# One transpose per group for the remaining columns with copies by DMA, and q and k in three chunks at a pitch of ten rows

## The chip, the cores and the metric

The kernel runs on one core of a Trainium2 chip. The metric is the time of one launch on the device, in microseconds; the kernel is fp32 throughout.

## The reference

The input x has 32 samples of 128 tokens and 144 channels, and each sample has a conditioning vector c of 144. Four stages follow each other; what matters is:

```python
# stage L0 (then L2, L3 alike, without the layernorm of q and k)
mod = silu(c) @ w_mod + b_mod                    # shift, scale, gate for attention and MLP
h = ln(x) * (1 + sc_msa) + sh_msa                # a row of scale and shift per sample
q, k, v = split(h @ w_qkv + b_qkv)               # 16 heads of 9 channels
q, k = ln(q), ln(k)                              # L0 only
attn = softmax(q @ k.T * 9 ** -0.5)
x = x + g_msa * ((attn @ v) @ w_proj + b_proj)
h = ln(x) * (1 + sc_mlp) + sh_mlp
x = x + g_mlp * (gelu(h @ w1 + b1) @ w2 + b2)    # hidden width 576
# stage L1, between L0 and L2: a rotation in a 64-dimensional subspace
U = qr(P); R = expm(A(silu(c) @ W.T + b))        # one R per sample
x = x + ((x @ U) @ R - x @ U) @ U.T
# stage L3: the MLP is a mixture of 4 experts, the two with the largest gate logits
x = x + g_mlp * sum(weight[e] * expert[e](h))
```

## The kernel before

**Tiling.** All of x stays in SBUF (x_sb, 128 tokens by 32 samples by 144). The code calls the three attention stages layers 0 (L0), 1 (L2) and 2 (L3); the rotation is worked in ahead of each group of layer 1. Four samples make a group (G = 4, eight groups per layer). Channels are contracted on TensorE's partitions, and 144 does not fit into 128: the channels are cut into CM = 128 main columns and CR = 16 remaining columns. So each normalised sample is turned twice: `xh` (128 columns) and `xr` (the 16 remaining columns, written four times at a distance of 32 by POOL, L638), by two transposes (L655, L656) into one bank, from which ACT makes `hM` and `hR` with the modulation as scale and bias (L658). In `hR` all four strips of 32 partitions hold the same 16 rows, so that the products of the remaining columns (contraction 32) run in four row groups of the array side by side: for four output chunks of q and k, for three of fc1, and for the samples of v. `both` (L663, L668) issues main and rest products of several banks, in the order that its caller asks for; a `yield` between the halves lets other work stand between them.

**q and k in layers 1 and 2.** `qk_chunks` (L700) makes q and k transposed, channels on partitions and the group's 512 tokens on columns, in four chunks of 128 weight columns (two of q, two of k). A strip of 32 rows of a chunk holds two heads in slots of 16 rows: a row of ones or of the largest score, and the 9 channels. ACT copies the chunks into `qT` and `kT` (L714, L721). `qk_mask` makes two copies of k with the other head's rows set to zero (r = 0 in place, r = 1 beside it), half of them on POOL (L734), half on ACT (L732).

**Scores.** `scores(s, w, n)` (L823, matmuls at L856) issues in one call the scores of half the heads of sample s, whose row maxima DVE takes (nm, L861), and for the sample before, w, the same scores again, transposed, with the maximum subtracted, which ACT exponentiates (L868). `weigh` (L883) multiplies with the values, `project_out` (L947) projects, and `residual` takes DVE's product with the gate (L936) and POOL's addition to x_sb (L933).

**The order.** Nothing is scheduled at run time or by a planner: the program order is written out by hand and each engine works through its own part of it in order. Time is counted in ticks. In tick t one sample's scores are computed, the sample before is weighed and the one before that is finished. A tick has named gaps, in this order in layers 1 and 2: a, e, t, the first call of scores, stats, weigh, b0, b, den, pre1, the second call of scores, c, y1, y2, y3, z, d. `put(tick, gap, f, ...)` places a piece of work in a gap, `put2` its two halves in two gaps. With t0 the tick in which group n of a layer starts (`first[layer] + 4 * n`), the pieces that matter are placed so:

- ln_stats of sample i for attention at tick t0+i-6 (layer 0: t0+i-5), and its turn `ln_T` at gap b of the next tick, in layer 2 at gap d of the same tick; for the MLP at ticks t0+i+3 (layer 0: t0+i+4)
- qk_chunks at tick t0-2, gap c; the masks at tick t0-1, POOL's at gap a and ACT's at b0; in layer 2 from group 3 on all four masks on POOL at gap z of the two ticks before t0
- values (v) at ticks t0 and t0+1, fc1 (`mlp1`) at t0+8 and t0+9 in layer 1, t0+10 and t0+11 in layer 0, and the experts' in layer 2 (`moe1`) from t0+8 on; `mlp2` two ticks after fc1's start

DMAs are issued by SP in program order: the inputs, the weights of later layers, one load of gates per group and kind (L305), the output.

Of the kernel before, what the change touches and what calls it, by code (L numbers as in the profile page):

```python
# [62 lines left out]
K_END = K_ONES + D  # L63
# [3 lines left out]
def tile_kernel(ctx: ExitStack, tc: tile.TileContext, a: dict, out: bass.AP):  # L67
# [27 lines left out]
    rmask = cst[:, K_MASK : K_MASK + 2]  # L95
    x_sb = const.tile([128, B, C], F32, name="x_sb")
# [144 lines left out]
    take_xr = ring([128, 128], "xr", 7, zeros)  # L241
    take_nm = ring([128, 128], "nm", 2, zeros)
# [18 lines left out]
    modM, modR = [], []  # L261

    def modulations(n):
        w = w_mods[n]
        mm = const.tile([128, 4, B], F32, name=f"modM{n}")
        mr = const.tile([128, 4, B], F32, name=f"modR{n}")
# [14 lines left out]
        nc.vector.tensor_scalar_add(mr[:, 2:, :], ps[:, 6:8, :], 1.0)  # L281
        modM.append(mm)
        modR.append(mr)

# [28 lines left out]
    uR = const.tile([128, D], F32, name="uR")  # L313
# [4 lines left out]
    def prep_qr():  # L318
# [69 lines left out]
        nc.vector.tensor_copy(ur[:, :CR], uT[:D, CM:])  # L388
# [6 lines left out]
        nc.vector.tensor_copy(uR, ps[:, 1, :])  # L395
# [223 lines left out]
    def ln_stats(pairs):  # L619
# [12 lines left out]
        for k, (s, kind) in enumerate(pairs):  # L632
            b = of(s)[1]
            minus, r = rs[:, 1, k : k + 1], rs[:, 0, k : k + 1]
            xh = work.tile([128, CM], F32, tag="xh", name=f"xh_{kind}_{s}", bufs=3)
            nc.gpsimd.tensor_scalar(xh, x_sb[:, b, :CM], minus, r, ALU.add, ALU.mult)
            xr = take_xr()
            nc.gpsimd.tensor_scalar(  # L638
                xr.rearrange("p (k c) -> p k c", k=4)[:, :, :CR],
                x_sb[:, b, CM:].unsqueeze(1).to_broadcast([128, 4, CR]),  # L640
                minus, r, ALU.add, ALU.mult,
            )
            st[s][f"xh_{kind}"], st[s][f"xr_{kind}"] = xh, xr

    def ln_T(s, kind):

        layer, b, g, i = of(s)
        if i == 0:
            for k in ("hM", "hR"):
                gr[g][f"{k}_{kind}"] = work.tile(  # L650
                    [128, G, T], F32, tag=f"{k}_{kind}", name=f"{k}_{kind}_{s}"
                )
# [3 lines left out]
        nc.tensor.transpose(ps[:, 1, :], st[s].pop(f"xr_{kind}"), ident)  # L656
        for k, m in (("hM", modM[layer]), ("hR", modR[layer])):
            nc.scalar.activation(  # L658
                gr[g][f"{k}_{kind}"][:, i, :], ps[:, k == "hR", :], AF.Identity,
                bias=m[:, sh, b : b + 1], scale=m[:, sc, b : b + 1],  # L660
            )

# [9 lines left out]
    def by_token(g, kind, i0, n, w, wR, name, rest_first=False):  # L672


        hM, hR = gr[g][f"hM_{kind}"], gr[g][f"hR_{kind}"]
# [3 lines left out]
            [(ps, hR[rows4(i), i0 + i, :], wR[rows4(i)]) for i, ps in enumerate(pss)],  # L679
# [13 lines left out]
    def qk_tiles(g):  # L693
        if "qT" not in gr[g]:
            name = f"{g[0]}_{g[1]}"
            gr[g]["qT"] = work.tile([128, 2, G * T], F32, tag="qT", name=f"qT_{name}")
            gr[g]["kT"] = work.tile([128, 4, G * T], F32, tag="kT", name=f"kT_{name}")
        return gr[g]["qT"], gr[g]["kT"]

    def qk_chunks(g):  # L700
# [5 lines left out]
        pss = [bank([128, G * T], f"ps_qk_{g[0]}_{g[1]}_{m}") for m in range(4)]  # L706
        cols = [slice(128 * m, 128 * m + 128) for m in range(4)]
# [5 lines left out]
        for t in range(2):  # L713
            nc.scalar.copy(qT[:, t, :], pss[t])  # L714
        if g == (1, 0):
            for t in range(2):
                nc.scalar.mul(kT[:, 2 + t, :], pss[2 + t], rmask[:, 1:2])
            gr[g]["k"] = kT, pss[2:]
        else:
            for t in range(2):  # L720
                nc.scalar.copy(kT[:, t, :], pss[2 + t])  # L721

    def qk_masked(g):
        kT, ks = gr[g].pop("k")
        for t, k in enumerate(ks):
            nc.vector.tensor_scalar(kT[:, t, :], k, rmask[:, 0:1], None, ALU.mult)

    def qk_mask(g, eng, t, r):
        kT = gr[g]["kT"]
        o, k, m = kT[:, 2 * r + t, :], kT[:, t, :], rmask[:, r : r + 1]  # L730
# [95 lines left out]
    def scores(s, w, n):  # L826
# [3 lines left out]
        if s is not None:  # L830
            layer, b, g, i = of(s)
            qT, kT = gr[g]["qT"], gr[g]["kT"].rearrange("p (r t) n -> p r t n", t=2)
            cols = slice(i * T, (i + 1) * T)
            ps = [bank([128, 4 * T], f"ps_s_{s}_{n}_{e}") for e in range(2)]
            if n == 0:
                st[s]["nm"] = take_nm()
            for t in range(2):
                for e in range(2):
                    rows = rows4(2 * n + e)
                    o = ps[e].rearrange("p (r t k) -> p r t k", r=2, t=2)[:, :, t, :]  # L840
                    mm[0].append((o, qT[rows, t, cols], kT[rows, :, t, cols]))
        if w is not None:
# [4 lines left out]
            for k in range(4):  # L847
                for e in range(2):
                    rows = rows4(2 * (1 - n) + e)
                    mm[1].append((pw[e][:, k * T : (k + 1) * T], kT[rows, k, cols], q2[rows, k % 2, :]))  # L850

        order = []
        for t in range(2):
            order += mm[0][2 * t : 2 * t + 2] + mm[1][4 * t : 4 * t + 4]
        for o, x, y in order:
            nc.tensor.matmul(o, x, y, start=True, stop=True)  # L856
        if s is not None:
            nmv = st[s]["nm"].rearrange("p (q s) -> p q s", s=SLOT)
            for e, view in enumerate(ps):
                at0 = 4 * n + 2 * e  # L860
                nc.vector.tensor_reduce(  # L861
                    nmv[:, at0 : at0 + 2, ONE : ONE + 2],
                    view.rearrange("p (r t k) -> p r t k", t=2, k=T), AX.X, ALU.max, negate=True,
                )
# [123 lines left out]
    def rotate_T(n):  # L988

        xM = work.tile([128, G, T], F32, tag="xM", name=f"xM_{n}", bufs=1)  # L990
        xR = work.tile([128, G, T], F32, tag="xR", name=f"xR_{n}", bufs=1)
# [4 lines left out]
        ps = bank([128, G, T], f"ps_xR_{n}")  # L996
        for i in range(G):
            xr = take_xr()
            nc.gpsimd.tensor_copy(xr[:, :CR], x_sb[:, n * G + i, CM:])
            nc.tensor.transpose(ps[:, i, :], xr, ident)  # L1000
# [3 lines left out]
    def rotate_in(n):  # L1004
        xM, xR = gr.pop(("rot", n))
        ps = bank([128, 2, T], f"ps_z_{n}")
        for u, x in ((uM, xM), (uR, xR)):
            for h in range(2):
                nc.tensor.matmul(  # L1009
# [575 lines left out]
```

## Time and profile before

| | |
|---|---|
| median of 3 runs | 1312.52 us (1311.24 to 1313.37) |
| profiled execution | 1303.81 us |
| its span in the trace | 1302.1 us |
| busy: PE, ACT, DVE, POOL | 1259.5, 833.4, 807.7, 690.4 us |
| starts of layer 1's and layer 2's first q and k products | 430.7 and 729.4 us |
| one group in layer 1, in layer 2 (distance of q and k products) | about 38.9 and 65.6 us |
| TensorE clock granted, mean | 0.993 |

PE is TensorE's matmul, PEld its weight load, DVE VectorE, ACT ScalarE, POOL GpSimd, SP the engine that issues DMAs. "Busy" is the time in which an engine ran instructions; L numbers are lines of the kernel before. In rows of the profile a tile's name stands before "<-" and its operands after; x is the count.

### The profile page before, as it was taken

To read this page: it belongs to the slowest core of one execution; us is meant where nothing else is said; L and a number is where in the kernel's file an instruction comes from. 1 tells how busy PE (TensorE), PEld (TensorE's weight loads), DVE (VectorE), ACT (ScalarE), POOL (GpSimd) and SP (SyncE) were. 2 spreads that over 40 slices of the span, in tenths; PEclk is the share of its full clock that TensorE was granted. 3 is DMA by queue.
4 is the path that set the end of the run, shared out by engine and by line. 5 is a ranking of instruction groups with operands and counts; after the bars stand their busy time and mean duration, and the time that the engine had idled before them with its cause. 6 is when DMAs were issued, how large, how long until landed. Compare 5 with 4: busy or idle time off the path is not lost.

```text
span 1302.1 us, 35663 instructions
## 1 busy us (share of the span) xinstructions
PE 1259.5 (97%) x14180; PEld 920.3 (71%) x14180; DVE 807.7 (62%) x2534; ACT 833.4 (64%) x1832; POOL 690.4 (53%) x1667
## 2 busy tenths in 40 slices
PE   6989898999999999999999999999999999999998
PEld 4678676786776667767777766767676767677666
DVE  5698888876774457667666666646464646455343
ACT  3568677678767566777767777665656555555431
POOL 5667777665753345445445554746464636361610
PEclk9999999999999999999999999999999999999999
DMA  8200000000003000000110000200000000000000
GB/s 234 62 2 21 20 7 15 20 3 22 20 2 134 19 11 21 11 20 20 37 29 20 20 11 11 76 11 19 11 20 11 19 11 19 11 19 2 19 10 10
DMA packets 21720, 34.43 MB, mean 26 GB/s; under 512 B 2353, under 2 KB 12497, under 8 KB 21297
## 3 DMA queue, kind: packets, MB, share of 16 engines
q1 hardware_dynamic: 20896, 31.70, 8.1%
q8 instruction: 114, 1.87, 0.6%
q10 hardware_dynamic: 656, 0.42, 0.2%
q14 instruction: 54, 0.43, 0.1%
HBM read 29.65 MB, written 2.47 MB: 25 GB/s over the span
## 4 chain that ended last, share of the span: by engine, by line
PE 71%; DVE 3%; ACT 1%; issue 0%; POOL 0%; DVEq 0%; POOLq 0%
PE ps_h L668 19%; PE ps_f L1118 10%; PE ps_s L856 7%; PE ps_qk L668 6%; PE ps_w L856 6%; PE ps_o L883 5%; PE ps_f L977 5%; PE ps_pj L947 3%; PE ps_v L668 2%; PE ps_f L1123 1%; PE ps_o L815 1%; DVE nm L861 1%; PE ps_z L1009 1%; PE ps_hT_m L656 1%; PE ps_cw L1106 1%; PE ps_hT_m L655 1%
## 5 line engine op out<-in xcount | busy, mean ns | idle before, releaser
L861 DVE TENSOR_REDUCE nm<-ps_s 128x4 f32<-128x512 f32 x384 | 246.3, 682 | 89.4 <-PE ps_w L856 67.8
L868 ACT ACTIVATE pr<-ps_w 128x512 f32<-128x512 f32 x384 | 208.6, 595 | 106.1 <-PE ps_w L856 104.6
L856 PE MATMUL ps_s<-kT,qT 32*128 32x256 f32 x1536 | 228.4, 404 | 0.7 <-ACT kT L791 0.6
L856 PE MATMUL ps_w<-q,kT 32*128 32x128 f32 x3072 | 229.0, 283 | 0.0
L856 PEld LDWEIGHTS ps_w<-q,kT 32*128 32x128 f32 x3072 | 194.2, 187 | 9.8 <-issue 6.2
L971 ACT ACTIVATE hid<-ps_h 128x512 f32<-128x512 f32 (+1 forms) x224 | 120.0, 591 | 100.1 <-PE ps_h L668 99.6
L856 PEld LDWEIGHTS ps_s<-kT,qT 32*128 32x128 f32 x1536 | 134.5, 184 | 29.6 <-issue 8.6
L668 PE MATMUL ps_h<-hM_m,mlps 128*128 128x512 f32 x304 | 144.0, 607 | 0.0
L1127 DVE SCALAR_TENSOR_TENSOR acc<-ps_f,cw,acc 128x144 f32<-128x144 f32 x128 | 46.7, 366 | 149.5 <-PE ps_f L1118 74.3
L933 POOL TENSOR_TENSOR x_sb<-x_sb,res_a 128x144 f32<-128x144 f32 x96 | 47.1, 490 | 146.7 <-DVE res_a L936 145.9
L883 PE MATMUL ps_o<-pr,vaug 128*32 128x128 f32 x3072 | 104.2, 276 | 0.3 <-issue 0.3
L883 PEld LDWEIGHTS ps_o<-pr,vaug 128*32 128x32 f32 x3072 | 78.1, 109 | 33.4 <-PE ps_w L856 18.9
L668 PEld LDWEIGHTS ps_h<-hM_m,mlps 128*128 128x128 f32 x304 | 53.3, 189 | 67.5 <-issue 66.6
L734 POOL TENSOR_SCALAR kT<-kT,cst 128x512 f32<-128x512 f32 x40 | 62.4, 1564 | 61.5 <-ACT kT L721 60.5
L977 PE MATMUL ps_f<-mlps,hid 128*128 128x144 f32 x640 | 93.5, 293 | 0.0
L977 PEld LDWEIGHTS ps_f<-mlps,hid 128*128 128x128 f32 x640 | 82.4, 191 | 7.8 <-issue 3.2
L868 ACT ACT_TABLE_LOAD x57 | 73.1, 1283 | 6.5 <-PE ps_w L856 5.7
L629 POOL TENSOR_SCALAR rs_m_a<-mv_m_a 128x2 f32<-128x2 f32 x81 | 15.6, 193 | 114.4 <-DVE mv_m_a L627 86.1
L968 ACT ACT_TABLE_LOAD x58 | 74.4, 1283 | 1.0
L658 ACT ACTIVATE hM_m<-ps_hT_m,modM 128x128 f32<-128x128 f32 x96 | 44.7, 465 | 45.5 <-PE ps_hT_m L656 45.4
L1118 PEld LDWEIGHTS ps_f<-pair,hid 128*128 128x128 f32 x512 | 66.9, 190 | 8.4 <-issue 7.7
L1118 PEld LDWEIGHTS ps_f<-mlps,hid 128*128 128x128 f32 x512 | 66.7, 190 | 8.1 <-issue 7.2
(328 smaller groups left out, 2918.5 us busy)
## 6 DMA issues: line engine op xcount, KB each, us to landing
gates<-gates SPq DMA_DIRECT2D x48, 288.0 KB, 3.5
x_sb<-in_x SPq DMA_DIRECT2D x8, 288.0 KB, 9.2
out_x<-x_sb SPq DMA_DIRECT2D x7, 288.0 KB, 2.5
mlps<-in_L_mlp SPq DMA_DIRECT2D x2, 1000.0 KB, 6.2
pair<-in_L_mlp SPq DMA_DIRECT2D x1, 1800.0 KB, 11.8
mlps<-in_L_mlp SPq DMA_DIRECT2D x1, 1800.0 KB, 8.2
pow<-in_W SPq DMA_DIRECT2D x4, 320.0 KB, 6.5
mlps<-in_L_wmod SPq DMA_DIRECT2D x4, 290.0 KB, 4.8
```

The source lines that it names most:

```text
L668: nc.tensor.matmul(ps, x, y, start=k == 0, stop=k == 1)
L734: eng.tensor_scalar(o, k, m, None, ALU.mult)
L856: nc.tensor.matmul(o, x, y, start=True, stop=True)
L861: nc.vector.tensor_reduce(nmv[:, at0 : at0 + 2, ONE : ONE + 2], view.rearrange("p (r t k) -> p r t k", t=2, k=T), AX.X, ALU.max, negate=True,)
L868: nc.scalar.activation(pr[:, 4 * e : 4 * e + 4, :].rearrange("p s q -> p (s q)"), view, AF.Exp, scale=SCALE,)
L883: nc.tensor.matmul(po[rows4(j), t, :], v[:, 4 * j + 2 * t + r, :], prs[j // 2][:, 4 * (j % 2) + 2 * r + t, :], start=r == 0, stop=r == 1,)
L933: nc.gpsimd.tensor_tensor(x_sb[:, b, :], x_sb[:, b, :], t, ALU.add)
L968: nc.scalar.activation(t, half, AF.Gelu_apprx_tanh)
L971: nc.scalar.activation(hid[:n, i], ps[:n], AF.Gelu_apprx_tanh)
L977: nc.tensor.matmul(ps, hid[:, at0, i, :], w2[:, m, :], start=m == 0, stop=m == NFC - 1)
L1118: nc.tensor.matmul(ps[:, 0, :], hid[:, at0 + m, i, :], w2[:, at0 + m, :], start=m == 0, stop=m == 3)
L1127: nc.vector.scalar_tensor_tensor(acc, ps[:, 0, :], w, acc, ALU.mult, ALU.add)
```

## The change

There are two parts.

**The remaining columns of a group.** (All but layer 0's attention, whose `hR` stays as it was.) POOL writes the 16 remaining columns of each of the four samples into one tile of the group, at columns 0, 32, 64 and 96 (`xg`). The tile is turned by one transpose, with the group's last sample, and ACT makes one tile `hG` from it, whose strips of 32 rows belong to the four samples; `modG` holds scale and shift in the same arrangement. `hR`, in which every strip must hold all four samples, is then made from `hG` by DMAs from SBUF to SBUF, each 32 x 128 (16 KB): 16 for attention, 12 for the MLP, all issued by SP. The values and the gate's logits read `hG` itself. The rotation likewise turns a group's remaining columns at once (`rotate_T`) and contracts each sample with its own strip of a zero-padded `uR`. In layer 1 the turn of a group's last sample stands at gap d of tick t0-3, where it stood at gap b of t0-2.

**q and k in three chunks.** In layers 1 and 2 a strip of 32 rows holds three heads at a pitch of ten rows (a row of ones and 9 channels). The first chunk is q and the second k of three heads of each strip; the third holds q and k of the fourth head. The fourth head's k is moved to its rows in `kT` by four DMAs of 9 x 512. Three masked copies of the second chunk are made: r = 1 by POOL at gap a, r = 2 by ACT at b0, r = 0 in place by POOL at gap c of tick t0-1 (layer 2 from group 3 on: all three by POOL at z). In `scores` the score products of a strip cover 384 and 128 columns, where they covered 256 twice. `kT` comes from a ring of two tiles whose fourth part is filled once, the tiles for the maxima are zeroed again ahead of layer 1, and weights and masks are laid out anew.

The diff, cut to its core:

```diff
-    take_xr = ring([128, 128], "xr", 7, zeros)
-    take_nm = ring([128, 128], "nm", 2, zeros)
+    take_xr = ring([128, 128], "xr", 3, zeros)
+    take_xg = ring([128, 128], "xg", 4, zeros)
+    nms = []
+
+    def fill_nm(t):
+        zeros(t)
+        nms.append(t)
+
+    take_nm = ring([128, 128], "nm", 2, fill_nm)
+    take_kT = ring([128, 4, G * T], "kT", 2, lambda t: None)
...
+        mg = const.tile([128, 4, NG], F32, name=f"modG{n}")
+        for i in range(G):
+            nc.gpsimd.tensor_copy(
+                mg[rows4(i)], mr[rows4(i)].rearrange("p k (g i) -> p k g i", i=G)[:, :, :, i]
+            )
...
-            xr = take_xr()
-            nc.gpsimd.tensor_scalar(
-                xr.rearrange("p (k c) -> p k c", k=4)[:, :, :CR],
-                x_sb[:, b, CM:].unsqueeze(1).to_broadcast([128, 4, CR]),
-                minus, r, ALU.add, ALU.mult,
-            )
-            st[s][f"xh_{kind}"], st[s][f"xr_{kind}"] = xh, xr
+            if (layer, kind) == (0, "a"):
+                xr = st[s]["xr_a"] = take_xr()
+                to = xr[:, :CR]
+            else:
+                if i == 0:
+                    gr[g][f"xr_{kind}"] = take_xg()
+                to = gr[g][f"xr_{kind}"][:, 32 * i : 32 * i + CR]
+            nc.gpsimd.tensor_scalar(to, x_sb[:, b, CM:], minus, r, ALU.add, ALU.mult)
+            st[s][f"xh_{kind}"] = xh
 
     def ln_T(s, kind):
 
         layer, b, g, i = of(s)
+        single = (layer, kind) == (0, "a")
         if i == 0:
-            for k in ("hM", "hR"):
+            for k in ("hM", "hR") if single else ("hM",):
                 gr[g][f"{k}_{kind}"] = work.tile(
                     [128, G, T], F32, tag=f"{k}_{kind}", name=f"{k}_{kind}_{s}"
                 )
         sh, sc = (SH_A, SC_A) if kind == "a" else (SH_M, SC_M)
         ps = bank([128, 2, T], f"ps_hT_{kind}_{s}")
         nc.tensor.transpose(ps[:, 0, :], st[s].pop(f"xh_{kind}"), ident)
-        nc.tensor.transpose(ps[:, 1, :], st[s].pop(f"xr_{kind}"), ident)
-        for k, m in (("hM", modM[layer]), ("hR", modR[layer])):
+        todo = [(gr[g][f"hM_{kind}"][:, i, :], modM[layer], b)]
+        if single:
+            nc.tensor.transpose(ps[:, 1, :], st[s].pop("xr_a"), ident)
+            todo.append((gr[g]["hR_a"][:, i, :], modR[layer], b))
+        elif i == G - 1:
+            nc.tensor.transpose(ps[:, 1, :], gr[g].pop(f"xr_{kind}"), ident)
+            hG = work.tile([128, T], F32, tag=f"hG_{kind}", name=f"hG_{kind}_{s}", bufs=1)
+            gr[g][f"hG_{kind}"] = hG
+            todo.append((hG, modG[layer], g[1]))
+        for k, (to, m, c) in enumerate(todo):
             nc.scalar.activation(
-                gr[g][f"{k}_{kind}"][:, i, :], ps[:, k == "hR", :], AF.Identity,
-                bias=m[:, sh, b : b + 1], scale=m[:, sc, b : b + 1],
-            )
+                to, ps[:, k, :], AF.Identity,
+                bias=m[:, sh, c : c + 1], scale=m[:, sc, c : c + 1],
+            )
+        if not single and i == G - 1:
+            hR = work.tile([128, G, T], F32, tag=f"hR_{kind}", name=f"hR_{kind}_{s}")
+            gr[g][f"hR_{kind}"] = hR
+            for m in range(4 if kind == "a" else 3):
+                for j in range(G):
+                    nc.sync.dma_start(hR[rows4(m), j, :], hG[rows4(j)])
...
-        hM, hR = gr[g][f"hM_{kind}"], gr[g][f"hR_{kind}"]
+        hM, hG = gr[g][f"hM_{kind}"], gr[g][f"hG_{kind}"]
         pss = [bank([128, w.shape[1]], f"{name}_{i0 + i}") for i in range(n)]
         yield from both(
             [(ps, hM[:, i0 + i, :], w) for i, ps in enumerate(pss)],
-            [(ps, hR[rows4(i), i0 + i, :], wR[rows4(i)]) for i, ps in enumerate(pss)],
+            [(ps, hG[rows4(i0 + i)], wR[rows4(i0 + i)]) for i, ps in enumerate(pss)],
...
-        pss = [bank([128, G * T], f"ps_qk_{g[0]}_{g[1]}_{m}") for m in range(4)]
-        cols = [slice(128 * m, 128 * m + 128) for m in range(4)]
+        pss = [bank([128, G * T], f"ps_qk_{g[0]}_{g[1]}_{m}") for m in range(3)]
+        cols = [slice(128 * m, 128 * m + 128) for m in range(3)]
         yield from both(
             [(ps, p.wqk[:, c], hM) for ps, c in zip(pss, cols)],
             [(ps, p.wqkR[rows4(m), cols[m]], hR[rows4(m)]) for m, ps in enumerate(pss)],
             False,
         )
-        for t in range(2):
-            nc.scalar.copy(qT[:, t, :], pss[t])
+        nc.scalar.copy(qT[:, 0, :], pss[0])
+        if g[0] == 1 and g[1] < 2:
+            nc.gpsimd.tensor_copy(kT[:, 3, :], kmask[:, 3:4].to_broadcast([128, G * T]))
         if g == (1, 0):
-            for t in range(2):
-                nc.scalar.mul(kT[:, 2 + t, :], pss[2 + t], rmask[:, 1:2])
-            gr[g]["k"] = kT, pss[2:]
+            for r in (1, 2):
+                nc.scalar.mul(kT[:, r, :], pss[1], kmask[:, r : r + 1])
+            gr[g]["k"] = kT, pss[1]
         else:
-            for t in range(2):
-                nc.scalar.copy(kT[:, t, :], pss[2 + t])
+            nc.scalar.copy(kT[:, 0, :], pss[1])
+        nc.scalar.copy(qT[:, 1, :], pss[2])
+        for j in range(4):
+            r = 32 * j + 1
+            nc.sync.dma_start(
+                kT[r : r + HD, 3, :], qT[r + PITCH : r + PITCH + HD, 1, :]
+            )
 
     def qk_masked(g):
-        kT, ks = gr[g].pop("k")
-        for t, k in enumerate(ks):
-            nc.vector.tensor_scalar(kT[:, t, :], k, rmask[:, 0:1], None, ALU.mult)
-
-    def qk_mask(g, eng, t, r):
+        kT, k = gr[g].pop("k")
+        nc.vector.tensor_scalar(kT[:, 0, :], k, kmask[:, 0:1], None, ALU.mult)
+
+    def qk_mask(g, eng, r):
         kT = gr[g]["kT"]
-        o, k, m = kT[:, 2 * r + t, :], kT[:, t, :], rmask[:, r : r + 1]
+        o, k, m = kT[:, r, :], kT[:, 0, :], kmask[:, r : r + 1]
...
                     rows = rows4(2 * n + e)
-                    o = ps[e].rearrange("p (r t k) -> p r t k", r=2, t=2)[:, :, t, :]
-                    mm[0].append((o, qT[rows, t, cols], kT[rows, :, t, cols]))
+                    if layer == 0:
+                        o = ps[e].rearrange("p (r t k) -> p r t k", r=2, t=2)[:, :, t, :]
+                        y = pair[rows, :, t, cols]
+                    else:
+                        ks = slice(3 * t, 3 + t)
+                        o = ps[e].rearrange("p (r k) -> p r k", r=4)[:, ks, :]
+                        y = kT[rows, ks, cols]
...
+        m = 6 if max(s or 0, w or 0) >= B else 4
+        order = mm[0][:2] + mm[1][:m] + mm[0][2:] + mm[1][m:]
...
+        ps = bank([128, T], f"ps_xR_{n}")
+        xr = take_xg()
+        nc.gpsimd.tensor_copy(
+            xr.rearrange("p (i c) -> p i c", i=G)[:, :, :CR], x_sb[:, n * G : n * G + G, CM:]
+        )
+        nc.tensor.transpose(ps, xr, ident)
...
+        for i in (0, 2, 1, 3):
+            h = i // 2
+            nc.tensor.matmul(
+                ps[h * D : (h + 1) * D, i % 2, :], uR[:, i, :], xR, start=False, stop=i % 2 == 1
+            )
...
-        for w, h in ((L3.wgate, hM), (L3.wgateR, hR)):
-            for i in range(G):
-                nc.tensor.matmul(ps[rows4(i)], w, h[:, i, :], start=h is hM, stop=h is hR)
+        for i in range(G):
+            nc.tensor.matmul(ps[rows4(i)], L3.wgate, hM[:, i, :], start=True, stop=False)
+        for i in range(G):
+            nc.tensor.matmul(
+                ps[rows4(i)], L3.wgateR[:, 32 * i : 32 * i + 32], hG, start=False, stop=True
+            )
...
-                    put(*((at_a, "d") if at_a != t0 + i - ahead else (at_a + 1, "b")), ln_T, s, "a")
+                    end = at_a != t0 + i - ahead or (layer, i) == (1, G - 1)
+                    put(*((at_a, "d") if end else (at_a + 1, "b")), ln_T, s, "a")
...
-                for r in (1, 0):
-                    if layer == 2 and n > 2:
-                        for t in range(2):
-                            put(t0 - 2 + (r == 0), "z", qk_mask, g, nc.gpsimd, t, r)
-                    elif g != (1, 0):
-                        put(t0 - 1, "a", qk_mask, g, nc.gpsimd, 0, r)
-                        put(t0 - 1, "b0", qk_mask, g, nc.scalar, 1, r)
+                if layer == 2 and n > 2:
+                    for r in (1, 2, 0):
+                        put(t0 - 2 + (r == 0), "z", qk_mask, g, nc.gpsimd, r)
+                elif g != (1, 0):
+                    put(t0 - 1, "a", qk_mask, g, nc.gpsimd, 1)
+                    put(t0 - 1, "b0", qk_mask, g, nc.scalar, 2)
+                    put(t0 - 1, "c", qk_mask, g, nc.gpsimd, 0)
...
+    put(first[1] - 2, "a", lambda: [zeros(t) for t in nms])
...
+    for r in range(3):
+        c[p % 32 // PITCH == r, K_M3 + r] = 1.0
+    c[p % 32 == 3 * PITCH, K_M3 + 3] = 1.0
...
-            to = ((128 * ht + 32 * hj + SLOT * hr)[:, None] + d).ravel()
-            n = 256
+            k = 2 * hr + ht
+            last = k == 3
+            at0 = 32 * hj + np.where(last, 256, PITCH * k)
+            to = ((at0 + 1)[:, None] + d).ravel()
+            n = 192
```

## The prediction

> **What bounds the kernel now.** I read the head of the page first, then the chain of work that ended last:
>
> ```profile
> PE 1259.5 (97%) x14180; PEld 920.3 (71%) x14180; DVE 807.7 (62%) x2534; ACT 833.4 (64%) x1832; POOL 690.4 (53%) x1667
> PE 71%; DVE 3%; ACT 1%; issue 0%; POOL 0%; DVEq 0%; POOLq 0%
> ```
>
> No engine but PE is near its span, and the chain (followed back only to 325 us) is nearly all PE. Whether that holds in each stage is told by the windows view (span, then busy time per engine, PE first, then clock, DMA share, GB/s), cut at the starts of the layers:
>
> ```profile
> 0.00:325.00 325.00, 296.00 (x4120) 230.63 (x4120) 253.86 (x889) 220.79 (x607) 220.40 (x637) 0.97 0.15 41
> 430.00:729.00 299.00, 297.52 (x3510) 211.32 (x3511) 189.20 (x540) 214.45 (x421) 141.26 (x314) 1.00 0.07 21
> 729.00:1302.00 573.00, 566.62 (x5394) 400.94 (x5386) 297.79 (x879) 324.95 (x624) 270.64 (x546) 1.00 0.06 17
> ```
>
> Layer 1 (430 to 729 us) leaves PE idle for 1.5 of 299 us, layer 2 for 6.4 of 573, layer 0 for about 9% of its time. So in layers 1 and 2 each PE slot removed is worth its length, and each wait put before a PE instruction costs its length. The clock is 1.00 there and drops out of the sum.
>
> **PE work removed.** The timeline of PE in one group of layer 1 (start, duration, line, tile, count):
>
> ```profile
> 578.56 3.70 PE L668 MATMUL ps_qk<-hM_a,L_wqk 128*128 128x512 f32 x8
> 582.19 1.14 PE L668 MATMUL ps_qk<-hR_a,L_wqkR 32*128 32x512 f32 x8
> ...
> 584.65 0.27 PE L655 MATMUL ps_hT_m<-cst,xh_m 128*128 128x128 f32 x1
> 584.76 0.27 PE L656 MATMUL ps_hT_m<-cst,xr 128*128 128x128 f32 x1
> 584.87 0.53 PE L947 MATMUL ps_pj<-L_wproj,oT 128*128 128x144 f32 x3
> ```
>
> Instructions are pipelined, so a slot is the distance between starts. A transpose holds 0.11 us (584.65, .76, .87). Three of four L656 transposes go for "m" in layer 0 (24), for "a" and "m" in layers 1 and 2 (96), and three of four in the eight rotations (24): 144 x 0.109 = **15.7 us**. The four main chunks of q and k take 582.19 - 578.56 = 3.63 us, so one chunk is 0.907; 16 groups x 0.907 = **14.5 us**. The rest chunks run side by side in four row groups (1.07 us to the next start); three of them need as long as four. I take off 0.8 us for layer 0, where part of the slots only widens a gap: **-29.4 us**.
>
> Taken at nothing: scores split into 384 + 128 columns instead of 256 + 256 (every row group keeps its total, a call stays at about 1.10 us), the rotation's four matmuls of 128 columns for two of 256, and the gate's logits. ACT (120 fewer hR of 0.345 us pitch, 16 copies of k fewer), and POOL's narrower xr (64 to 16 columns) gain nothing by themselves, because PE's own work hides both; if PE's order were looser in layer 0 they might give 1 us. In layer 1 the turn of a group's fourth sample moves from gap "b" of tick t0-2 to "d" of t0-3: two transposes and two ACT operations. Layer 2 has its turns at "d" already and PE loses 0.9 us in all there on inputs from POOL (xh, x_sb: 0.5 and 0.4 us before L655 in the view of that line, over the whole span), so I take it at nothing, at most 0.1 us a group. The set-up (small copies for the grouped modulation, a larger memset) costs at most 1 us in layer 0: **+1**.
>
> **The mask that now stands late.** Before, POOL masked k's first half (both r) at gap "a" one tick ahead and ACT the second half. Now POOL does r=1 at "a", ACT r=2, and POOL r=0 in place at gap "c" of that tick. In POOL's order this puts the last one behind the residual add of the tick's mlp2, which waits for DVE's res_m, which waits behind the two reductions nm. Then the next tick's first scores on PE wait for the mask. The timelines of DVE, POOL and PE (PEld is its weight load) there, and the group of the masks (busy, mean ns):
>
> ```profile
> 592.10 0.30 DVE L936 TENSOR_TENSOR res_m<-ps_f,gates 128x144 f32<-128x144 f32 x1
> ...
> 592.74 0.94 POOL L933 TENSOR_TENSOR x_sb<-x_sb,res_m 128x144 f32<-128x144 f32 x2
> ...
> 592.80 0.70 PE L856 MATMUL ps_s<-kT,qT 32*128 32x256 f32 x4
> ...
> 594.33 0.81 PEld L883 LDWEIGHTS ps_o<-pr,vaug 128*32 128x32 f32 x32
> ...
> L734 POOL TENSOR_SCALAR kT<-kT,cst 128x512 f32<-128x512 f32 x40 | 62.4, 1564 | 61.5 <-ACT kT L721 60.5
> ```
>
> Allowing for POOL's shorter work ahead, the add starts at 592.48, the mask after 0.45 us at 592.93, and ends 1.56 us later at 594.49. PE wants the scores at 592.80 less the removed transpose. Nothing behind them can pass: w, values and weigh are in order on the same queue. The weighing comes 1.4 us late (about 595.65 for 594.22, the call's own 1.10 us after the mask). This holds for groups 2 to 7 of layer 1 (6 x 1.43 = 8.6) and groups 0 to 2 of layer 2 (1.5, 1.2, 1.1). Group 0 of layer 1 is masked by DVE, in group 1 POOL is free early, and from group 3 of layer 2 masks stand at "z": **+12.4**. Bounds: 0 if POOL takes it ahead of the add, 15 if nothing overlaps.
>
> **Copies before q and k.** hR comes by 12 DMAs (16 for "a"). SP's pitch and a small transfer's landing are in the timeline and the DMA rows (KB each, us from issue to landing):
>
> ```profile
> 395.26 0.43 SPq L106 DMA_DIRECT2D L_wgate<-in_L_wgate  x1
> 395.73 0.43 SPq L106 DMA_DIRECT2D L_wgateR<-in_L_wgateR  x1
> ...
> gates<-gsb SPq DMA_DIRECT2D x6, 18.0 KB, 1.5
> ```
>
> The twelfth 16 KB copy lands 11 x 0.47 + 1.6 = 6.8 us after hG. In layer 1 hG would end near 574.0 and the rest start at 581.15: 7.1 us, 6.9 less hG's eight lane waits, so the stall is 0.25 us for seven groups; the gap is 6.3 us in groups 0 to 2 of layer 2 (0.75 each) and 6.1 in group 0 of layer 1 (about 1); later groups have 16.9 us. **+4.8**, between 0 and 11 x 1.4 + 4.8 = 20 if a copy took 1.4 us longer. "m" has over a tick (9 us) of slack. The 64 copies of the fourth head's k land under later ticks' work. SP also loads the gates (L305), one load in about 18 us: one queued behind 16 copies comes 7.5 us later and is read four ticks after; the copies themselves stand more than a tick behind the load ahead of them, whose wait ended at 592.43 in the example. The Trainium skill, page "DMA: Bandwidth & Descriptors", section "Anatomy of one DMA — SWDGE (gpsimd) path", speaks against many small copies: it gives each about 2.0 us of fixed cost whatever its size, measured on GpSimd's path. This case's row has 1.5 us for 18 KB on SP; by the page some eleven groups would lose 0.4 us more, 4 to 5 us in all.
>
> **Semaphores on PE.** Each group of copies arrives on eight semaphores. A PE instruction that waits for n of them carries n-1 waiting instructions on PE's queue; the trace has five in a row at 428.98, 429.09, 429.19, 429.30 and 429.41, so 0.106 us each. The three rest products of fc1 (24 groups, rest first) wait for one or two engines now, and then also for four copies each: 12 to 14 such instructions, 1.3 to 1.5 us, though all have long landed. PE's queue runs ahead of its array by only 0.8 to 0.95 us there, after the scores call (records for the products at 597.21 start at 596.44). So the array stands still for about 0.8 us in layer 1, 0.6 in layers 0 and 2, less in layer 0's gaps: 8 x 0.8 + 8 x 0.62 + 8 x 0.47 = **+15**. Bounds: 0 if satisfied waits are cheaper than those five, 17 with layer 0 in full. Before q and k's rest 2.7 us of main products hide them.
>
> **Sum.** -29.4 + 1 + 12.4 + 4.8 + 15 = +3.8 on the profiled execution's 1303.81 us: 1307.6. The median of 1312.52 is 0.67% above that execution; scaled, **1316 us**.
>
> **Rivals.**
> 1. Faster. The waits at fc1 are covered, because one that is already satisfied holds PE's queue for little more than the 0.051 us of its record: 13 of them take 0.7 us, inside the lead. It decides from about 0.9/13 = 0.07 us downwards. For it: "issue" carries 0% of the chain. Against: the pitch of 0.106 and the short lead. -29.4 + 1 + 12.4 + 4.8 = -11.2, so 1292.6; scaled about 1301, and 1297 if the copies also come in time.
> 2. Slower by late copies. SP's queue becomes the place: a copy from SBUF to SBUF lands after 3 us instead of 1.6. For it: larger transfers in the same rows take 2.5 us and more; against: the 18 KB row. Eleven groups have no slack left, so each tenth of a us over the row costs 1.1: at 3 us 1.4 x 11 = 15 more, about 1331.
> 3. No change. Half of the semaphore cost is hidden (7.5 for 15): -3.7, so 1300.1, scaled 1309; up to 1313 as the copies' wait moves within its bounds.
>
> **How the numbers follow.** Forecast 0.40, rival 1 0.30, rival 2 0.18, rival 3 0.12. A difference of 0.2% (2.6 us) is about what a measurement of this kernel can tell. Faster: 0.30 + 0.01. Same: 0.04 of the forecast's lower end and 0.09 of rival 3. Slower: 0.36 + 0.18 + 0.02. The range 1297 to 1332 reaches to rival 1 with its copies in time and just past rival 2, and leaves out the far tails of both (0.10 and 0.08); the forecast's own is 1310 to 1322.
>
> **What would show it.** PE: 144 fewer transposes and 32 fewer products ps_qk; PE busy lower by some 29 us. The mask: PE idle before ps_s released by POOL kT, about 1.4 us in nine groups. The copies: idle before ps_qk's rest, released by SP. The semaphores: PE idle before ps_h<-hR_m put down to "issue", 0.5 to 0.8 us in each of 24 groups. Wrong if the idle before ps_h is under 5 us or the idle before ps_qk above 15.

## The result, and the profile after

The changed kernel takes 1342.91 us (median of 4 runs, 1335.93 to 1349.84); the kernel before, run beside it, 1311.88. The ratio is 1.0245, with a 95% interval of 1.0202 to 1.0288: slower by 2.4%, where 1316 us was forecast (0.3%) and the range ended at 1332. The profiled execution took 1339.11 us with a span of 1337.4; before it was 1303.81 and 1302.1.

The head of the page, the first line of its chain of waits, and the row of the granted clock:

```profile
PE 1266.1 (95%) x14004; PEld 921.6 (69%) x14004; DVE 807.1 (60%) x2536; ACT 777.0 (58%) x1687; POOL 679.2 (51%) x1655
...
PEclk9789999999999999989989899999999999999999
...
PE 59%; SPq 6%; DVE 3%; ACT 3%; POOL 2%; DMA 1%; issue 1%; ACTq 0%; DVEq 0%; POOLq 0%
```

PE has 176 instructions fewer (144 transposes less, 64 records of q and k's products less, two to a product, and 32 of the rotation's more), but is busy 6.6 us longer. The chain, nearly all PE before, now goes through SP's queue (the copies) and POOL. The clock row has eights in its middle, where before there were only nines. The windows view from one group's q and k products to the next (span, busy time per engine with PE first, then clock, DMA share, GB/s) shows two groups of layer 1 and one from late in layer 2:

```profile
545.40:585.90 40.50, 38.33 (x467) 27.36 (x463) 25.06 (x72) 25.14 (x48) 18.47 (x40) 1.00 0.11 29
585.90:630.80 44.90, 41.52 (x467) 29.74 (x463) 25.05 (x72) 25.14 (x48) 18.51 (x40) 0.92 0.09 26
1030.70:1095.00 64.30, 64.30 (x623) 45.65 (x620) 34.00 (x103) 36.26 (x68) 33.00 (x67) 1.00 0.09 24
```

The last of them is what was hoped for: 64.3 us where a group took 65.6. The same group of layer 1 took 38.9 before; the first takes 1.6 more at full clock, the second 6.0 more at a mean clock of 0.92. What PE waits for in layers 1 and 2 (the view of waits: us in total, times, longest):

```profile
PE ps_s L907 <- POOL kT L778: 15.1, 9, 1.8
PE ps_qk L707 <- DMA hR_a<-hG_a: 12.0, 11, 1.5
```

Both waits are seen at work in the chain of one group (start, length, what ran):

```profile
588.20 0.59 SPq L700
588.79 0.38 issue
589.17 1.82 DMA hR_a<-hG_a
590.99 0.27 issue
591.26 1.80 PE ps_qk L707 x2
...
604.23 0.46 POOL x_sb L988
604.73 0.49 POOL x_sb L988
605.22 1.56 POOL kT L778
606.77 0.04 issue
606.82 0.39 PE ps_s L907
```

The twelfth copy is issued at 589.17 and lands 1.82 us later, when PE has had nothing to do since its main products. The mask stands behind two residual adds and ends at 606.78; PE's scores follow. And after the first wait, the windows view in steps of 1 us:

```profile
590.00:591.00 1.00, 0.00 (x0) 0.00 (x0) 0.00 (x0) 0.92 (x2) 0.00 (x0) 1.00 0.08 18
591.00:592.00 1.00, 0.74 (x1) 0.29 (x2) 0.00 (x0) 0.00 (x0) 0.00 (x0) 0.75 0.13 31
592.00:593.00 1.00, 1.00 (x3) 0.02 (x2) 0.00 (x0) 0.00 (x0) 0.00 (x0) 0.50 0.12 29
...
597.00:598.00 1.00, 1.00 (x13) 0.82 (x15) 0.31 (x1) 0.13 (x1) 0.33 (x1) 0.50 0.08 18
598.00:599.00 1.00, 1.00 (x28) 0.88 (x26) 0.10 (x1) 0.00 (x0) 1.00 (x2) 0.83 0.07 17
```

PE stood still for 1.4 us, and from 591.51 to 598.33, with work all the time, it had half its clock. The trace's clock records in layers 1 and 2 hold nine such stretches, each 3.41 or 6.83 us long, 37.5 us together; before there were none.

**Where the time went.** The time up to layer 1's first q and k products is no measure of the change: in the thirteen profiled executions of this study it lies anywhere between 428.2 and 444.3 us, and in the five kernels whose layer 0 is that of before at 430.7, 431.0, 435.0, 440.4 and 444.1. So traces are compared from those products to the end of the span ("layers 1 and 2"): 871.4 us before, 904.2 after, 32.8 more. A stretch at half clock costs at most half its length. Each ratio is to the kernel before as it ran beside that kernel (medians 1307.1 to 1311.9 us).

| kernel | median, us | ratio to before (95%) | layers 1 and 2, us | at half clock there, us |
|---|---|---|---|---|
| before | 1311.88 | | 871.4 | 0 |
| changed | 1342.91 | 1.0245 (1.0202 to 1.0288) | 904.2 | 37.5 |
| masks early | 1323.89 | 1.0148 (1.0087 to 1.0208) | 891.9 | 20.5 |
| through DRAM | 1304.26 | 0.9990 (0.9952 to 1.0028) | 867.7 | 13.7 |
| both edits | 1288.85 | 0.9832 (0.9762 to 0.9902) | 847.2 | 0 |
| both edits, again | 1287.17 | 0.9816 (0.9771 to 0.9860) | 847.2 | 0 |
| both, MLP's copies as changed | 1308.33 | 0.9978 (0.9935 to 1.0021) | 874.8 | 20.5 |
| both, attention's copies as changed | 1323.22 | 1.0084 (1.0047 to 1.0120) | 890.6 | 37.5 |
| first part alone | 1300.78 | 0.9946 (0.9915 to 0.9977) | 863.0 | 0 |
| second part alone | 1294.97 | 0.9876 (0.9819 to 0.9934) | 854.8 | 0 |
| before, half a mask late | 1315.67 | 1.0034 (1.0002 to 1.0066) | 878.9 | 0 |
| before, a mask late | 1328.44 | 1.0143 (1.0090 to 1.0196) | 890.8 | 13.7 |
| before, two masks late | 1351.54 | 1.0310 (1.0251 to 1.0368) | 916.8 | 41.0 |

### The profile page after: what moved, and what is told of

It is laid out like the page before. It is cut to its first block, busy times and chain, and to the rows that moved or that the text cites. A ratio compares the mean times of both kernels' runs of the same rounds, so it can differ in the third digit from the quotient of the medians.

```text
span 1337.4 us, 36183 instructions
## 1 busy us (share of the span) xinstructions
PE 1266.1 (95%) x14004; PEld 921.6 (69%) x14004; DVE 807.1 (60%) x2536; ACT 777.0 (58%) x1687; POOL 679.2 (51%) x1655
## 3 DMA queue, kind: packets, MB, share of 16 engines
q1 hardware_dynamic: 48160, 41.62, 11.1%
## 4 chain that ended last, share of the span: by engine, by line
PE 59%; SPq 6%; DVE 3%; ACT 3%; POOL 2%; DMA 1%; issue 1%; ACTq 0%; DVEq 0%; POOLq 0%
PE ps_h L707 17%; PE ps_f L1180 9%; SPq L700 6%; PE ps_s L907 5%; PE ps_w L907 5%; PE ps_o L938 5%; PE ps_f L1032 3%; PE ps_v L707 2%; PE ps_qk L707 2%; PE ps_pj L1002 2%; DMA hR_a<-hG_a 1%; PE ps_f L1185 1%; POOL kT L778 1%; DVE nm L919 1%; ACT pr L923 1%
## 5 line engine op out<-in xcount | busy, mean ns | idle before, releaser
L907 PE MATMUL ps_s<-kT,qT 32*128 32x256 f32 (+2 forms) x1536 | 235.5, 410 | 15.7 <-POOL kT L778 15.1
L907 PE MATMUL ps_w<-q,kT 32*128 32x128 f32 x3072 | 233.4, 286 | 0.0
L907 PEld LDWEIGHTS ps_w<-q,kT 32*128 32x128 f32 x3072 | 197.4, 190 | 10.3 <-issue 6.3
L907 PEld LDWEIGHTS ps_s<-kT,qT 32*128 32x128 f32 x1536 | 137.8, 188 | 45.3 <-POOL kT L778 16.9
L938 PE MATMUL ps_o<-pr,vaug 128*32 128x128 f32 x3072 | 108.9, 285 | 0.0
L938 PEld LDWEIGHTS ps_o<-pr,vaug 128*32 128x32 f32 x3072 | 81.6, 113 | 34.3 <-PE ps_w L907 18.5
L1032 PE MATMUL ps_f<-mlps,hid 128*128 128x144 f32 x640 | 98.0, 303 | 0.0
L1032 PEld LDWEIGHTS ps_f<-mlps,hid 128*128 128x128 f32 x640 | 86.5, 199 | 7.8 <-issue 3.4
L778 POOL TENSOR_SCALAR kT<-kT,cst 128x512 f32<-128x512 f32 x35 | 54.7, 1566 | 54.1 <-ACT kT L760 54.1
L988 POOL TENSOR_TENSOR x_sb<-x_sb,res_m 128x144 f32<-128x144 f32 x64 | 32.6, 510 | 89.7 <-DVE res_m L991 88.6
```

The costliest lines, as they stand in the source:

```text
L778: eng.tensor_scalar(o, k, m, None, ALU.mult)
L938: nc.tensor.matmul(po[rows4(j), t, :], v[:, 4 * j + 2 * t + r, :], prs[j // 2][:, 4 * (j % 2) + 2 * r + t, :], start=r == 0, stop=r == 1,)
L988: nc.gpsimd.tensor_tensor(x_sb[:, b, :], x_sb[:, b, :], t, ALU.add)
L1032: nc.tensor.matmul(ps, hid[:, at0, i, :], w2[:, m, :], start=m == 0, stop=m == NFC - 1)
```

## The experiments

The theory after the result: PE waits for the late mask and the late copies, and these waits halve its clock for a time that costs about as much again. The rivals: the clock falls for another reason (the traffic of the copies, chance), or the loss is in the waiting semaphores of the prediction.

**Masks early.**

```diff
-                    put(t0 - 1, "b0", qk_mask, g, nc.scalar, 2)
-                    put(t0 - 1, "c", qk_mask, g, nc.gpsimd, 0)
+                    put(t0 - 1, "a", qk_mask, g, nc.scalar, 2)
+                    put(t0 - 1, "a", qk_mask, g, nc.gpsimd, 0)
```

> The changed kernel with one edit: the three masks of a group (POOL r=1, ACT r=2, POOL r=0) all at gap a of tick t0-1, as POOL's two masks stood before, so that no mask is queued behind the residual adds. Theory (waits on PE cost their own length, and a wait of over about 1.7 us inside one window of 3.41 us also halves TensorE's clock for the windows after): the 15.1 us that PE waited for POOL's mask go, and with them 8 to 12 of the 24 us that half clock cost; about 1318 us beside 1343. Rival (the lower clock comes from the DMA copies or from chance, not from the waits): only the 15 go, about 1328 us, and the granted clock stays at 0.97. Rival (POOL is late in any case): no change.

Measured: 1323.89 us. The wait for POOL's mask is gone and the time at half clock falls from 37.5 to 20.5 us; in layers 1 and 2 that is 12.3 us and not 23 to 27, between the theory and the first rival. The waits of that run:

```profile
PE ps_qk L707 <- DMA hR_a<-hG_a: 11.5, 11, 1.5
PE ps_h L707 <- DMA hR_m<-hG_m: 2.1, 2, 1.7
```

The second line is new: fc1 now waits for the copies of the MLP's hR, which the mask's wait had covered. Set beside the run with both edits (PE's order is the same in both, so that each instruction's start can be compared), fc1's rest products lose 10.9 us in all, where the changed kernel loses 0.2.

**Through DRAM.**

```diff
-            for m in range(4 if kind == "a" else 3):
-                for j in range(G):
-                    nc.sync.dma_start(hR[rows4(m), j, :], hG[rows4(j)])
+            hD = dram.tile([128, T], F32, tag=f"hD_{kind}", name=f"hD_{kind}_{s}", bufs=2)
+            nc.sync.dma_start(hD, hG)
+            for m in range(3):
+                nc.sync.dma_start(hR[rows4(m)], hD.rearrange("(j p) t -> p j t", j=G))
```

> The changed kernel with one edit: hR made by 1 copy of hG to DRAM and 3 copies back (one per strip, all four samples at once), 4 DMAs for 16 or 12. Theory: with a pitch of 0.63 us and 1.8 us of landing, the third strip is there about 2.4 + 3 x 0.6 + 1.9 = 6 us after hG where it took 10; the 12 us before the rest products of q and k go, and 8 to 12 us of half clock; about 1321 us. Rival (waiting semaphores on PE are dear): some 10 us more go at fc1, about 1311. Rival (a return from DRAM takes 3 us or more): the wait stays, 1335 to 1345.

Measured: 1304.26 us, better than expected. In its view of waits only the mask is left of the two:

```profile
PE ps_s L908 <- POOL kT L779: 15.0, 9, 1.8
```

Layers 1 and 2 are 36.5 us shorter than in the changed kernel: 12.0 of waits, up to 11.9 of half clock (half of 37.5 less 13.7), and some 13 more. The view of waits gives only the time in which PE stands still. The three rest products otherwise start together; in the changed kernel the first two run side by side or nearly so, and the third starts 1.3 to 3.1 us after the first, when its strip has landed. Instruction by instruction, q and k's rest products lose 26.0 us over eleven groups in the changed kernel (those at half clock included) and nothing here. The rival of dear semaphores, with its 1311, is not the reason for the further gain: fc1's rest products lose only 0.2 us in the changed kernel. The edit changes two things at once, the number of copies and where they read from; no run separates these.

**Both edits.**

> Both edits: masks at gap a, and hR by 1 + 3 copies through DRAM. Theory: no long wait is left on PE, the granted clock returns to 0.99, and what stays is the removed work of 22 us: 1288 to 1295 us, faster than the kernel before. Rival (clock lowered by the copies): about 1311. Rival (the two waits cover each other, one goes and the other grows): 1315 to 1325.

Measured: 1288.85 us, ratio 0.9832. None of these waits is left and no stretch of half clock in layers 1 and 2: the removed work comes out, 24.2 us. This kernel beats both others.

**The kernel before with a late mask**, and nothing else of the change:

```diff
-                        put(t0 - 1, "a", qk_mask, g, nc.gpsimd, 0, r)
+                        put(t0 - 1, "a" if r else "c", qk_mask, g, nc.gpsimd, 0, r)
```

> The kernel before with one edit: POOL's in-place mask of the first half of k (r=0) at gap c of tick t0-1 instead of gap a, nothing else. Theory: PE waits some 1.4 us before the first scores in nine groups (13 us) and a few of these waits lower the clock (3 to 10 us): 1325 to 1335 us beside 1312. Rival (a wait of this length never lowers the clock): 1325 with a clock of 0.993. Rival (the mask is hidden in the tick): 1312.

Measured: 1328.44 us; four stretches at half clock, 13.7 us, in a kernel without these copies. One of them, in the windows view (the clock is the third number from the end):

```profile
525.00:526.00 1.00, 0.00 (x0) 0.00 (x0) 0.24 (x2) 0.64 (x2) 1.00 (x1) 1.00 0.39 141
...
529.00:530.00 1.00, 1.00 (x14) 0.61 (x6) 0.74 (x4) 0.37 (x1) 0.10 (x1) 0.50 0.00 0
530.00:531.00 1.00, 1.00 (x6) 0.77 (x4) 0.58 (x4) 0.00 (x0) 0.92 (x3) 0.50 0.00 0
```

This refutes the traffic as a cause that is needed. Layers 1 and 2 are 19.4 us longer: 13.9 at the scores that wait and 5.5 spread over what follows at half clock.

**Two masks late, and half a mask late**, as a measure of the wait's length. The mask at gap c was done twice, or for half of its columns (the others at gap a); cut to the lines that do it:

```diff
+                        if not r:
+                            put(t0 - 1, "c", qk_mask, g, nc.gpsimd, 0, r)
```

```diff
+                            put(t0 - 1, "a", qk_mask, g, nc.gpsimd, 0, r, slice(256, 512))
+                            put(t0 - 1, "c", qk_mask, g, nc.gpsimd, 0, r, slice(0, 256))
```

> The kernel before with the late mask of the run above, done twice in a row (the second changes nothing in the data), so that PE's nine waits are some 1.57 us longer each: 13.7 us of waiting become about 28. Theory (a wait that fills more than half of a window of 3.41 us halves the clock for the next one or two): nearly all nine waits of about 3 us now lower the clock, 15 to 30 us on top of the 28, granted clock about 0.98; in layers 1 and 2 some 43 to 58 us over the kernel before, 1350 to 1368. Rival (the lower clock has nothing to do with waits): 28 us, about 1337, clock 0.993.

> The kernel before with half of the late mask: POOL's in-place mask of r=0 at gap a for the first half of k's rows' columns 256 to 511, at gap c for columns 0 to 255 only. The late piece takes half of 1.56 us, so PE's nine waits are some 0.65 us each, 6 us in all. Theory (a wait lowers the clock only where it fills about half of a window of 3.41 us): no window in layers 1 and 2 is at half clock, about 1315 to 1318 us. Rival (each wait has a chance in proportion to its length): one or two windows at half clock, 2 to 4 us more.

Measured: 1351.54 and 1315.67 us. The line of the mask in the view of waits, for half a mask, one and two:

```profile
PE ps_s L856 <- POOL kT L734: 7.8, 9, 1.1
```

```profile
PE ps_s L856 <- POOL kT L734: 13.7, 9, 1.7
```

```profile
PE ps_s L856 <- POOL kT L734: 28.5, 9, 3.4
```

Nine waits of about 0.9 us cause no half clock, nine of 1.5 us four stretches, nine of 3.2 us nine. The times nearly add up: 878.9 is 871.4 + 7.5; 890.8 is 871.4 + 19.4, against 13.7 of waits and 6.8 for half of the time at half clock; 916.8 is 45.4 more, against 28.5 and 20.5. What goes beyond the waits, 5.7 and 16.9, is somewhat less than that half. The rival by proportion is not borne out by the half mask: none of its nine waits lowered the clock.

**The two parts alone**: the first with its hR through DRAM, the second with its masks at gap a.

> The kernel before with the first part alone (group transposes of the remaining columns, grouped modulation, turn of the fourth sample earlier in layer 1), its hR by 1 copy to DRAM and one per strip back; q and k stay in four chunks with the masks of before. Theory: no wait is added, so the 144 transposes go at 0.109 us, less what layer 0 hides: 12 to 15 us faster, in layers 1 and 2 (120 transposes with the rotation's) some 11 to 13 us from the first q and k products to the end. Rival (the transposes were hidden or are paid again by the copies): within 4 us of the kernel before.

> The kernel before with the second part alone (q and k in three chunks, scores in 384 and 128 columns, fourth head's k by four copies), its masks at gap a; hR and the transposes as before. Theory: 16 main chunks go at 0.907 us: 12 to 14.5 us faster, all of it in layers 1 and 2. Rival (scores of 384 and 128 columns are dearer than 256 and 256, or the rest of three chunks is): under 8 us faster.

Measured: ratios 0.9946 and 0.9876; in layers 1 and 2 8.4 and 16.6 us less, 25.0 together, against 24.2 for both at once. The first part falls short of its 11 to 13 us, the second exceeds its 14.5.

**The copies by kind**: both edits, but with the copies as in the changed kernel for the MLP alone, then for attention alone.

```diff
-            for m in range(3):
-                nc.sync.dma_start(hR[rows4(m)], hD.rearrange("(j p) t -> p j t", j=G))
+            for m in range(4 if kind == "a" else 3):
+                if kind == "m":
+                    nc.sync.dma_start(hR[rows4(m)], hD.rearrange("(j p) t -> p j t", j=G))
+                else:
+                    for j in range(G):
+                        nc.sync.dma_start(hR[rows4(m), j, :], hG[rows4(j)])
```

(This is attention's, cut: the copy to DRAM is made for the MLP alone. The MLP's has the two kinds exchanged.)

> Both edits of the fourth run, but hR for the MLP made by 12 copies from SBUF to SBUF as in the changed kernel (attention keeps 1 + 3 through DRAM). Theory: the copies land more than a tick ahead, so all that is added is waiting semaphores on PE before fc1's rest products; the trace of the run with masks early showed 0.5 to 0.6 us a group there: 5 to 12 us slower than the run with both edits, with no wait of PE for a DMA. Rival (satisfied semaphores are free): the same time as with both edits.

> Masks at gap a, hR for the MLP by 1 + 3 through DRAM, but hR for attention by 16 copies from SBUF to SBUF as in the changed kernel. Theory: the copies for attention come 1.3 us a group too late for the rest products of q and k in eleven groups (14 us), and some of these waits lower the clock (0 to 8 us): in layers 1 and 2 14 to 22 us over the run with both edits, about 1305 us. Rival (only the copies for the MLP matter, those for attention cost no more than the 4.8 us that the prediction gave): within 6 us of the run with both edits.

Measured: 1308.33 and 1323.22 us, 27.6 and 43.4 us more in layers 1 and 2 than with both edits. Neither went by its theory. The MLP's copies were thought early by more than a tick. In fact SP issues the first one 2.3 to 5.2 us after hG in most groups of layer 1, because the four copies of the fourth head's k (some 0.75 us each) stand ahead of them on its queue, in one group the weights of the last layer too; the twelfth, which has still to land, is issued between 2.0 us before and 1.5 us after fc1's first products start. Real waits, then, in place of the semaphores, and 20.5 us at half clock. Three of them in the view of waits:

```profile
PE ps_h L713 <- DMA hR_m<-hG_m: 3.1, 3, 1.4
```

The view puts four more, at the same third rest product, down to other engines; PE stands still there for 7.6 us in all. Attention's copies cost 28.7 us at q and k's rest products (some of it at half clock), and most of the remainder is work slowed by the 37.5 us at half clock. In these two runs half clock follows shorter waits than any late mask's: one of 0.70 us before a rest product of q and k (at 511.1 us), one of 0.86 us at fc1 (at 551.3). There the rest products ran two at a time before the wait and one alone after it. Whether the clock takes that for idleness, no run tests.

The two do not add to the changed kernel's loss, because there a wait for one (the mask, the copies of the other kind) covers another.

**Both edits, again.**

> The kernel with both edits once more, for a narrower interval of its ratio to the kernel before: 24 us less in layers 1 and 2 by the traces, so a ratio of 0.978 to 0.986.

Measured: ratio 0.9816, interval 0.9771 to 0.9860; layers 1 and 2 847.2 us. Head of its page, clock row and chain:

```profile
PE 1238.6 (96%) x14004; PEld 907.1 (71%) x14004; DVE 805.5 (63%) x2536; ACT 774.6 (60%) x1687; POOL 675.6 (53%) x1655
...
PEclk9689999999999999999999999999999999999999
...
PE 70%; DVE 3%; ACT 1%; issue 0%; POOL 0%; DVEq 0%
```

With the same 14004 instructions PE is busy 27.5 us less than in the changed kernel, and SP and POOL are out of the chain.

## Why the prediction was wrong

The sign was right, the size far off: 31 us for 3.5. The sign was in part luck: it rests on the 15 us of semaphores, which came to nothing, and without them the sum was -11.2.

In layers 1 and 2 the terms make +1.0 us (-27.6 of work, 12.4 for the mask, 4.8 for the copies, 11.4 of semaphores), and 32.8 was measured. Waits came to 27.1 (forecast 17.2), half clock to at most 18.8 (0), semaphores to about 0 (11.4), removed work to 24.2 (27.6). The remaining 11.1 or more had no term; the largest part of it that was found is rest products that ran without their full width (below). By the steps:

**"The clock is 1.00 there and drops out of the sum"** is the step that failed. It held for the kernel before, which has no wait of that length in layers 1 and 2; the change adds twenty. 37.5 us at half clock cost up to 18.8 us, about half of the loss there, and the late masks in the kernel before show that the wait alone does it. The clock records come in multiples of 3.413 us. So the time from layer 1's first q and k products to 970 us was cut into windows of that length, in step with the records, and PE's idle time in each window at full clock was taken from the starts and modelled ends of its instructions. In the four kernels in which only masks came late (the three of before, and the one through DRAM), 17 of the 18 windows with 1.7 us or more of idle time were followed by one at half clock, and none of the 19 with 1.0 to 1.7 us; so whether a wait of 1.5 us is punished depends on whether it falls into one window or across the edge of two. In the changed kernel it was five of five, and four of the twelve with less; these four hold a wait for the copies, as do the windows with 0.6 to 0.9 us that were punished in the runs by kind. The Trainium skill, page "TensorE: Matmul & The Clock Gate", section "Part 1: The HAM clock gate (the "warmup" mystery)", describes this gate: a free-running window of 3413 ns and, for a core that works alone, two states of the clock, half and full, which these records agree with (0.5 and 1.0 alone). It gives a whole idle window as the condition; by the late masks here half a window is enough.

**Copies before q and k, +4.8.** The place was right and the size was not: PE stood still for 12.0 us, and with the third rest product running alone, some of it at half clock, the loss at them was 26.0. (The term itself is not what its figures give: 6.8 us of landing against gaps of 6.9, 6.3 and 6.1 make 2.2, and the stalls that it names make 5.0.) SP's pitch was taken as 0.47 us from loads out of DRAM; a copy from SBUF to SBUF occupies the queue for 0.588 (median of 256) and follows at 0.63:

```profile
L700 SPq DMA_DIRECT2D hR_a<-hG_a x256: 507/588/1777, 430.2 to 1156.3; - x128
```

In the group shown the first copy is issued at 581.27 and the twelfth at 589.17, 7.9 us for the 5.2 of the sum (6.9 to 8.1 over the groups), and it lands in 1.82 us for 1.6. Rival 2 had this place and this kind of price (a slower copy, no slack in eleven groups), with the landing as its cause instead of the pitch.

**Slack for "m"** of over a tick was wrong too: the four copies of k ahead of them on SP were followed to the end of their own use, and not priced for what is queued behind them. In the changed kernel the mask's wait covers it.

**The mask, +12.4**: 15.1 us in nine waits, as forecast in place and number. POOL is behind for the reason given and also because its own normalisation before (xh, xg) ends at 604.23.

**Semaphores, +15**: about nothing; PE is never idle for 0.15 us or more before fc1's rest products in layers 1 and 2, which the prediction itself named as a sign of being wrong. In the changed kernel eight, not 12 to 14, of the waiting instructions precede them in most groups of layer 1, and six in layer 2, at the forecast pitch of 0.106 us but for one of 0.25 (610.03 to 610.99 in one group); the products start at 610.95, right behind the scores. Eight at that pitch take 0.85 us and fit the lead of 0.8 to 0.95. The cover of rival 1 was real, by their number and not by a shorter pitch.

**Removed work, -29.4**: of the 27.6 that belonged to layers 1 and 2, 24.2 came out once nothing stood in its way. The second part gave 16.6 for 14.5: 0.87 us a group at the chunk itself, near the forecast, about 0.1 more at the scores, and 1.4 and 2.2 us in all in the first two groups of layer 1. The first gave 8.4 for 13.1. In one group of layer 1, 0.98 us of transposes went and some 0.5 came out: 0.11 us was given back at the transpose of the maxima, where PE's idle time grew from 0.03 to 0.15 us, as much at the scores behind it, and the rest at later scores. Busy PE was taken for bound PE in slots that are not; the other groups were not followed in this way.

Layer 0 stays open: its 24 transposes, and its copies, are smaller than what separates two executions there.

## What to carry to other kernels

In layers 1 and 2 of the kernel before, TensorE was idle for 7.6 of 871 us and never at half clock. Late masks of 1.5 and 3.2 us there cost 1.4 and 1.6 times the wait, those of 0.9 us the wait alone; the late copies cost more than twice theirs, because the work beside them ran without its full width. So price a new wait in a kernel like this above its length, and look at what runs around it. Work is cheap to remove only if what replaces it (here the copies and the masks) lands before PE asks for it: count the queue ahead of it, at the pitch of that very kind of transfer.

## What the runs showed of the hardware

- A wait can lower the granted clock to one half for one or two windows of 3.41 us. Of the late masks in the kernel before, those of up to 1.1 us never did (0 of 9), those of 1.5 us on average in 4 of 9 cases, those of 3.2 us always (9 of 9). Around late copies, where part of the work runs on fewer row groups, waits of 0.7 and 0.9 us were followed by half clock too.
- A copy from SBUF to SBUF of 32 x 128 fp32 (16 KB) held SP's queue for 0.588 us; one of 64 KB out of DRAM into the same tile for 0.424 (medians). For attention's hR, one copy to DRAM and three back had their last issue 2.4 to 4.1 us after the first, the twelve copies 6.9 to 8.1.
- Late operands cost more than the time in which the engine stands still (26.0 us against 12.0): of three rest products that start together in row groups, the third started 1.3 to 3.1 us late and ran alone when its strip landed last.
